# Beta plus x for one group in four: from GpSimd additions to a pair of DMA transfers, with the b2 addition re-divided

## The chip, the core and the metric

The kernel runs on one core of one Trainium2 chip. The metric is the device time of one execution in microseconds (us); lower is better. The engines are TensorE (PE, with its weight loads PEld), VectorE (DVE), ScalarE (ACT), GpSimd (POOL) and SyncE (SP, which here only issues DMAs).

## The reference

`x` has 128 batches of 128 rows by 512 columns, in float32. Each batch `b` has a language id between 0 and 8 (the tables have ten rows), which chooses its weights:

```python
w1 = W1[language_ids]; w2 = W2[language_ids]
h = relu(einsum('bsh,bha->bsa', x, w1) + b1[language_ids][:, None, :])     # 512 -> 128
y = x + einsum('bsa,bah->bsh', h, w2) + b2[language_ids][:, None, :]       # 128 -> 512
mean, var = over the 512 columns of y
normed = (y - mean) * rsqrt(var + 1e-5)
out = x + normed * gamma[language_ids][:, None, :] + beta[language_ids][:, None, :]
```

## The kernel before, in words

All 128 rows of a batch lie on the 128 partitions, so one batch is a 128x512 tile. Input comes in groups of four batches (`G`, one DMA of 1 MB, `load_x`), output goes out in pairs (one DMA of 512 KB, `store`). W1, W2 and the rows of beta, gamma and b2 are held on the chip for all ten languages (`beta_b`, `gamma_b` and `b2_b` have each row copied to every partition), and each engine picks its slice with a register that holds the language id (`lid`).

The work on one batch `b`:

- TensorE transposes x (`transpose_x`, L218), ScalarE copies the transpose out (L222) and copies the batch's W1 to a buffer (`stage_w1`, L209). TensorE multiplies by W1 (`down`, L241), ScalarE adds b1 and applies relu (L249), TensorE multiplies by W2 (`up`, L258).
- The addition of b2 has three ways. For batches that `b2_by_matmul` names, TensorE adds it with one more matmul into the same PSUM tile (L257). For those of `b2_by_vector`, VectorE adds it in PSUM (L271). For all others GpSimd makes `r = x + b2` ahead of time (`add_b2`, L228).
- VectorE adds `r` (or x) to the product in PSUM and sums the row (`residual`, L273). ScalarE makes the sum of squares (L288), VectorE the statistics, then `(y - mean) * gamma` (`scale`, L322), and last `o = y * rstd + o` (`finish`, L331), where `o` already holds `x + beta`.
- That first content of `o`, `x + beta`, is made by GpSimd (`add_beta`, L235) for each batch.

The order on each engine is written out by hand: `keep` (L44) ties each instruction behind the one before it on its engine. Only the stores are issued outside it, so that the builder places them among SP's other DMAs. The main loop (L492) counts `i`, with `b = i - 3`. In the turn of `b`, GpSimd makes `r` of batch b+2 and `o` of batch b, TensorE does `up` of b+1, VectorE does `residual` of b, and `finish` follows three batches behind. For the last five batches (`E` = 123) the order differs: in the turn of 123 GpSimd makes everything that is left of `r` and `o`, and afterwards it takes part in the ends of batches 123, 124 and 125 (`by_pool`, L384 and L386: two multiplications by gamma and three additions, between ScalarE and the stores). The last six stores are of one batch each, and SP issues them in the order of the batches.

The buffers that count here: four `r` tiles (`rp`), so that GpSimd can make the fifth `r` only when VectorE's `residual` has used the first; five `o` tiles of two batches each (`op`), so that the sixth waits for the first one's store to land; five PSUM tiles for the product (`p_y`), so that TensorE's `up` of b+5 waits for `finish` of b; four x tiles of a group each.

Of the kernel before, what the change touches and what calls it, by code (L numbers as in the profile page):

```python
# [8 lines left out]
FP = mybir.dt.float32  # L9
# [3 lines left out]
ALU = mybir.AluOpType  # L13
ET = mybir.EngineType
PSUM = bass.MemoryType.PSUM

P = 128
G = 4
# [6 lines left out]
def cond_resid_kernel(ctx: ExitStack, tc: tile.TileContext, x, itok, W1, b1, W2, b2, gamma, beta, out):  # L25
# [8 lines left out]
    nc = tc.nc  # L34
    B, S, H = x.shape
    L, _, A = W1.shape
    KC = H // P
    NG = B // G
# [5 lines left out]
    def keep(ins):  # L44

        engine = ins.ins.engine
        if engine in last:
            tc.add_manual_dep(ins.ins, last[engine], behind, reason="kept order")
        last[engine] = ins.ins.name
        return ins  # L50
# [1 line left out]
    const = ctx.enter_context(tc.tile_pool(name="const", bufs=1))  # L52
    xp = ctx.enter_context(tc.tile_pool(name="xp", bufs=4))
    rp = ctx.enter_context(tc.tile_pool(name="rp", bufs=4))
    op = ctx.enter_context(tc.tile_pool(name="op", bufs=5))
    tp = ctx.enter_context(tc.tile_pool(name="tp", bufs=2))
    wp = ctx.enter_context(tc.tile_pool(name="wp", bufs=3))
    st = ctx.enter_context(tc.tile_pool(name="st", bufs=6))
# [5 lines left out]
    xs = {}  # L64

    def load_x(g):
        t = xp.tile([P, G, H], FP, tag="x", name=f"x_{g}")
        keep(nc.sync.dma_start(out=t, in_=x[g * G : (g + 1) * G].rearrange("b s h -> s b h")))
        xs[g] = t

    def xb(b):
        return xs[b // G][:, b % G, :]
# [27 lines left out]
    for l in range(0, L, 5):  # L100
        keep(
            nc.sync.dma_start(
                out=w1e[:, l : l + 5].rearrange("p l k a -> p l (k a)"),
                in_=W1[l : l + 5].rearrange("l (p k) a -> p l (k a)", k=KC),
# [4 lines left out]
    def load_w1(k):  # L109
        keep(  # L110
            nc.sync.dma_start(out=w1[:, :, k, :], in_=W1[:, k * P : (k + 1) * P, :].rearrange("l p a -> p l a"))
        )

    for l in range(0, L, 5):
        keep(
            nc.sync.dma_start(
                out=w2[:, l * H : (l + 5) * H].rearrange("p (l h) -> p l h", l=5),
                in_=W2[l : l + 5].rearrange("l a h -> a l h"),
# [48 lines left out]
    beta_b = const.tile([P, L * H], FP, name="beta_b")  # L167
# [14 lines left out]
    lids, xT, w1s, hT, rs, os, ys, ssqs, nmeans, rstds = {}, {}, {}, {}, {}, {}, {}, {}, {}, {}  # L182
    phs, pxs, sums = {}, {}, {}

    def lid(b, engine):
        g = b // G
        if (g, engine) not in lids:
            loads, vals = nc.values_load_multi_w_load_instructions(
                lang[0:1, g * G : (g + 1) * G],
                engines=[engine],  # L190
                min_val=0,
                max_val=L - 1,
                skip_runtime_bounds_check_because="clamped on the chip to 0..L-1 above",
            )
            for ins in loads:
                keep(ins)
            lids[g, engine] = vals
        return lids[g, engine][b % G]

    def b2_by_matmul(b):  # L200
        return b < 4 or (b % 4 == 1 and not b2_by_vector(b))

    def b2_by_vector(b):
        return b % 8 == 5 and 8 <= b < B - 16

    def stage_w1(b):
        w1s[b] = wp.tile([P, KC, A], FP, tag="w1s", name=f"w1s_{b}")
        src = (w1e if b < EARLY else w1).rearrange("p l k a -> p (l k a)")[:, bass.ds(lid(b, ET.Activation) * (KC * A), KC * A)]
        keep(nc.scalar.copy(w1s[b].rearrange("p k a -> p (k a)"), src))  # L209

    def transpose_x(b):
        pxs[b] = p_x.tile([P, KC, P], FP, tag="xT", name=f"pxT_{b}")
        for k in range(KC):
            if b < EARLY:
                cols = xb(b).rearrange("s (p k) -> s k p", k=KC)[:, k, :]
            else:
                cols = xb(b)[:, k * P : (k + 1) * P]
            keep(nc.tensor.transpose(pxs[b][:, k, :], cols, ident))  # L218

    def copy_xT(b):  # L220
        xT[b] = tp.tile([P, KC, P], FP, tag="xT", name=f"xT_{b}")
        keep(nc.scalar.copy(xT[b], pxs.pop(b)))  # L222

    def add_b2(b):
        if not b2_by_matmul(b) and not b2_by_vector(b):
            rs[b] = rp.tile([P, H], FP, tag="r", name=f"r_{b}")
            v = lid(b, ET.Pool)
            keep(nc.gpsimd.tensor_tensor(rs[b], xb(b), b2_b[:, bass.ds(v * H, H)], ALU.add))  # L228

    def add_beta(b):  # L230
        g, j = divmod(b, 2)
        if j == 0:
            os[g] = op.tile([P, 2, H], FP, tag="o", name=f"o_{g}")
        v = lid(b, ET.Pool)
        keep(nc.gpsimd.tensor_tensor(os[g][:, j, :], xb(b), beta_b[:, bass.ds(v * H, H)], ALU.add))  # L235

    def down(b):
        phs[b] = p_h.tile([P, P], FP, tag="h", name=f"ph_{b}")
        for k in range(KC):
            keep(  # L240
                nc.tensor.matmul(  # L241
                    phs[b], lhsT=w1s[b][:, k, :], rhs=xT[b][:, k, :], start=(k == 0), stop=(k == KC - 1)
                )
            )
        del xT[b], w1s[b]

    def relu(b):
        hT[b] = tp.tile([P, P], FP, tag="hT", name=f"hT_{b}", bufs=6)
        keep(nc.scalar.activation(hT[b], phs.pop(b), AF.Relu, bias=b1T[:, bass.ds(lid(b, ET.Activation), 1)]))  # L249

    def up(b):
        v = lid(b, ET.PE)
        ys[b] = p_y.tile([P, H], FP, tag="y", name=f"py_{b}")
        m = b2_by_matmul(b)
        if m:
            pick_b = pick[:, bass.ds(v + 2 * L, 1)].to_broadcast([96, P])
            keep(nc.tensor.matmul(ys[b], lhsT=pick_b, rhs=parts[:96, :], start=True, stop=False))  # L257
        keep(nc.tensor.matmul(ys[b], lhsT=hT[b], rhs=w2[:, bass.ds(v * H, H)], start=not m, stop=True))  # L258
        del hT[b]
# [5 lines left out]
    def residual(b):  # L265
        r = rs.pop(b) if b in rs else xb(b)
        if b % 2 == 0:
            sums[b // 2] = st.tile([P, 2], FP, tag="sum", name=f"sum_{b // 2}")
        if b2_by_vector(b):
            v = lid(b, ET.DVE)  # L270
            keep(nc.vector.tensor_tensor(ys[b], ys[b], b2_b[:, bass.ds(v * H, H)], ALU.add))  # L271
        keep(
            nc.vector.scalar_tensor_tensor(ys[b], ys[b], 1.0, r, ALU.mult, ALU.add, accum_out=col(sums, b))  # L273
        )
# [28 lines left out]
    def rstd_1(g):  # L303
        y0s[g] = p_s.tile([P, 6], FP, tag="s", name=f"stat_{g}")
        keep(nc.vector.reciprocal(y0s[g][:, 0:2], sds[g]))  # L305
# [32 lines left out]
    def on(b):  # L338
        return 0 <= b < B
# [152 lines left out]
    for i in range(3, B + U):  # L492
        b = i - U - 1
        if b > 0 and b % G == 0 and b // G + 3 < NG:
            load_x(b // G + 3)
        if i == 5:
            load_x(3)
        if i in (4, 6, 8, 10):
            load_w1((i - 4) // 2)
        if i == 4:  # L500
            up(2)
        if i == 5:
            up(3)
        if i > 3 and on(i):
            transpose_x(i)
        if b <= E:
            add_b2(b + 2)
            add_beta(b)
        if i > 4 and on(i - 1):
            down(i - 1)  # L510
        if i > 3 and on(i):
            copy_xT(i)
        if i > 4 and on(i + 1):
            stage_w1(i + 1)
        if i > 4 and on(i - 1):
            relu(i - 1)
        if i > 5 and on(i - U):
            up(i - U)


        g, half = divmod(b, 2)
        p = g - 1
        mine, old = 0 <= p < B // 2, 0 <= p - 1 < B // 2
        if b == E:
            add_b2(b + 3)
            add_beta(b + 1)
            add_b2(b + 4)
            for n in range(b + 2, B):
                add_beta(n)
        if b > E:  # L530
            tail(b)
        elif half == 0:
            if on(b):
                residual(b)
            if mine:
                rstd_1(p)
                scale(2 * p)
            if on(b):
                negative_mean(b)
            if mine:  # L540
                rstd_2(p)
            if old:
                finish(2 * p - 1)
                store(p - 1)
            if mine:
                rstd_3(p)
        else:
            if on(b):
                residual(b)
            if mine:  # L550
                rstd_4(p)
                scale(2 * p + 1)
            if on(b):
                negative_mean(b)
            if mine:
                finish(2 * p)
        if 0 <= b <= E:
            square(b)
            if half == 1:
                deviation(g)  # L560

        for n, engine in ((i + 3, ET.Activation), (i - U + 3, ET.PE), (b + 1, ET.DVE), (b + 5, ET.Pool)):
            if on(n):
                lid(n, engine)
# [37 lines left out]
```

## Time and profile before

| | before |
|---|---|
| median of 3 runs | 313.8 us (313.76 to 313.9) |
| the profiled execution: its own time, and its span | 313.83 us, 312.1 us |
| granted TensorE clock | 0.99 |
| PE busy | 300.5 us, 96% |
| DVE busy | 297.3 us, 95% |
| ACT busy | 285.4 us, 91% |
| POOL busy | 280.1 us, 90% |
| GpSimd additions: `r`, `o` | 93 of 1274 ns, 128 of 1274 ns |
| b2 matmuls on TensorE (L257), b2 additions on VectorE (L271) | 22 of 381 ns, 13 of 692 ns |
| DMA, mean | 242 GB/s, 75.49 MB |

The span runs from the first to the last instruction of the profiled execution; the other 1.73 us of its time lie around it. A matmul's duration in the profile reaches over the start of the next one, so that TensorE's pace is read from the distance between starts. The same holds for GpSimd and VectorE, whose instructions overlap a little. Times inside the span are counted from its start.

### The profile page before, as it was taken

Reading aid. Unit: us, or ns where it says so; the run is one execution under the profiler, and the core shown is the slowest. Engines: PE = TensorE matmul, PEld = TensorE weight load, DVE = VectorE, ACT = ScalarE, POOL = GpSimd, SP = SyncE. Lnnn points to the kernel's source line nnn. Section 1 sums busy time; section 2 is a strip of 40 time slices with the busy share of each in tenths; the row PEclk is TensorE's granted clock in tenths of the full one; section 3 lists DMA queues with packets and bytes.
Section 4 is the critical chain, followed back from the end, with each engine's and each line's share of the span. In section 5 each row is a group of like instructions: output and inputs, shape, how many; then the busy total and the mean of one; then the engine's idle time right before and its main releaser. Section 6 shows DMA issues by size and latency. Waiting matters only on the chain.

```text
span 312.1 us, 7096 instructions
## 1 busy us (share of the span) xinstructions
PE 300.5 (96%) x1869; PEld 223.8 (72%) x1869; DVE 297.3 (95%) x945; ACT 285.4 (91%) x724; POOL 280.1 (90%) x234
## 2 busy tenths in 40 slices
PE   8999999999999999999999999999999999999970
PEld 3567787777777767777777777777777777777740
DVE  6677999999999999999999999999999999999995
ACT  3878999999999999999999999999999999999982
POOL 1319978999999999999999999999999999999963
PEclk9999999999999999999999999999999999999995
DMA  6999998767776777667666567576666667633234
GB/s 209 387 387 352 326 339 275 238 229 226 236 250 225 255 265 269 242 231 270 257 227 226 210 238 253 213 272 269 232 232 198 232 247 239 244 134 138 88 149 168
DMA packets 42313, 75.49 MB, mean 242 GB/s; under 512 B 1785, under 2 KB 6916, under 8 KB 42274
## 3 DMA queue, kind: packets, MB, share of 16 engines
q1 hardware_dynamic: 42214, 75.00, 68.6%
q8 instruction: 15, 0.25, 0.3%
q14 instruction: 24, 0.20, 0.2%
q10 hardware_dynamic: 60, 0.05, 0.1%
HBM read 41.49 MB, written 33.55 MB: 240 GB/s over the span
## 4 chain that ended last, share of the span: by engine, by line
PE 91%; DVE 5%; ACT 1%; issue 1%; DVEq 1%; DMA 1%; ACTq 0%
PE ph L241 36%; PE py L258 34%; PE pxT L218 18%; PE py L257 1%; PE row L175 1%; DVE py L273 1%; DVE gamma_b L180 1%; DVE py L322 1%; DVE o L331 1%; DMA rows<-in_L_cond_b_dram 1%; ACT sq L366 0%; DVEq L597 0%; ACT n L382 0%; DVE left L156 0%; DVE left L154 0%
## 5 line engine op out<-in xcount | busy, mean ns | idle before, releaser
L235 POOL TENSOR_TENSOR o<-x,beta_b 128x512 f32<-128x512 f32 x128 | 161.6, 1274 | 12.8 <-ACT beta_b L178 9.2
L241 PE MATMUL ph<-xT,w1s 128*128 128x128 f32 x1024 | 135.6, 275 | 0.5 <-ACT w1s L209 0.5
L258 PE MATMUL py<-w,hT 128*128 x256 | 131.1, 594 | 0.0
L228 POOL TENSOR_TENSOR r<-x,b_b 128x512 f32<-128x512 f32 x93 | 118.5, 1274 | 11.5 <-DMA x<-in_x_dram 9.2
L241 PEld LDWEIGHTS ph<-xT,w1s 128*128 128x128 f32 x1024 | 124.7, 192 | 2.4 <-ACT w1s L209 1.0
L218 PEld LDWEIGHTS pxT<-ident,x 128*128 128x128 f32 x512 | 65.5, 148 | 64.9 <-issue 44.8
L322 DVE SCALAR_TENSOR_TENSOR py<-py,nmean,gamma_b 128x512 f32<-128x512 f32 x126 | 93.8, 745 | 0.2 <-issue 0.2
L331 DVE SCALAR_TENSOR_TENSOR o<-py,rstd,o 128x512 f32<-128x512 f32 x122 | 91.0, 746 | 0.0
L288 ACT ACTIVATE sq<-py,sum 128x512 f32<-128x512 f32 x124 | 85.3, 688 | 1.4 <-DVE py L273 1.3
L222 ACT COPY xT<-pxT 128x512 f32<-128x512 f32 x128 | 73.8, 577 | 9.8 <-PE pxT L218 6.3
L218 PE MATMUL pxT<-ident,x 128*128 128x128 f32 x512 | 77.4, 274 | 0.0
L209 ACT COPY w1s<-w 128x512 f32 x112 | 69.5, 621 | 0.0
L273 DVE SCALAR_TENSOR_TENSOR py<-py,r 128x512 f32<-128x512 f32 x93 | 64.6, 694 | 1.3 <-PE pxT L218 0.6
L249 ACT ACTIVATE hT<-ph,b1T 128x128 f32<-128x128 f32 x128 | 47.4, 370 | 1.0 <-PE ph L241 1.0
L258 PEld LDWEIGHTS py<-w,hT 128*128 128x128 f32 x256 | 40.6, 192 | 2.4 <-ACT hT L249 0.7
L273 DVE SCALAR_TENSOR_TENSOR py<-py,x 128x512 f32<-128x512 f32 x35 | 24.4, 697 | 1.6 <-ACT sq L288 0.6
L288 ACT ACTIVATION_READ_ACCUMULATOR sq<-py,sum 128x1 f32 x124 | 25.7, 208 | 0.0
L299 ACT ACTIVATE sd<-ssq,eps 128x2 f32<-128x2 f32 x62 | 18.3, 296 | 2.1
L279 DVE TENSOR_SCALAR nmean<-sum 128x1 f32<-128x1 f32 x128 | 19.5, 152 | 0.1
L305 DVE RECIPROCAL stat<-sd 128x2 f32<-128x2 f32 x62 | 13.0, 210 | 1.0 <-ACT sd L299 1.0
L273 DVE DVE_READ_ACCUMULATOR py<-py,r 128x1 f32 x93 | 13.4, 144 | 0.0
L317 DVE RECIPROCAL rstd<-stat 128x2 f32<-128x2 f32 x62 | 10.4, 168 | 0.0
(56 smaller groups left out, 120.6 us busy)
## 6 DMA issues: line engine op xcount, KB each, us to landing
out_dram<-o SPq DMA_DIRECT2D x61, 512.0 KB, 3.9
x<-in_x_dram SPq DMA_DIRECT2D x30, 1024.0 KB, 5.8
w1e<-in_L_cond_W_dram SPq DMA_DIRECT2D x2, 1280.0 KB, 8.7
w<-in_L_cond_W_dram SPq DMA_DIRECT2D x2, 1280.0 KB
w<-in_L_cond_W_dram SPq DMA_DIRECT2D x4, 640.0 KB, 15.2
x<-in_x_dram SPq DMA_DIRECT2D x4, 512.0 KB, 8.4
out_dram<-o SPq DMA_DIRECT2D x6, 256.0 KB, 2.0
rows<-in_L_cond_beta_dram ACTq DMA_DIRECT2D x1, 20.0 KB
```

The source lines that it names most:

```text
L209: keep(nc.scalar.copy(w1s[b].rearrange("p k a -> p (k a)"), src))
L218: keep(nc.tensor.transpose(pxs[b][:, k, :], cols, ident))
L222: keep(nc.scalar.copy(xT[b], pxs.pop(b)))
L228: keep(nc.gpsimd.tensor_tensor(rs[b], xb(b), b2_b[:, bass.ds(v * H, H)], ALU.add))
L235: keep(nc.gpsimd.tensor_tensor(os[g][:, j, :], xb(b), beta_b[:, bass.ds(v * H, H)], ALU.add))
L241: nc.tensor.matmul(phs[b], lhsT=w1s[b][:, k, :], rhs=xT[b][:, k, :], start=(k == 0), stop=(k == KC - 1))
L249: keep(nc.scalar.activation(hT[b], phs.pop(b), AF.Relu, bias=b1T[:, bass.ds(lid(b, ET.Activation), 1)]))
L258: keep(nc.tensor.matmul(ys[b], lhsT=hT[b], rhs=w2[:, bass.ds(v * H, H)], start=not m, stop=True))
L273: nc.vector.scalar_tensor_tensor(ys[b], ys[b], 1.0, r, ALU.mult, ALU.add, accum_out=col(sums, b))
L288: nc.scalar.activation(sq, ys[b], AF.Square, bias=col(sums, b), scale=-float(H), accum_out=col(ssqs, b))
L322: nc.vector.scalar_tensor_tensor(ys[b], ys[b], col(nmeans, b), gamma_b[:, bass.ds(v * H, H)], ALU.add, ALU.mult)
L331: nc.vector.scalar_tensor_tensor(o, ys.pop(b), rstds[g][:, j : j + 1], o, ALU.mult, ALU.add)
```

## The change

Every fourth group of batches (q = 3, 7, ... 27, so 7 groups and 28 batches) gets its `x + beta` without GpSimd arithmetic. SP issues four DMAs that copy the rows of beta from `beta_b` to a tile `od` of four batches (`fill_beta`, in the turn five batches ahead of the group), and GpSimd issues one DMA of 1 MB that adds the group's x to that tile as it lands (`add_x`, two batches ahead). The `od` pool has one tile. The pool of `o` tiles goes from five to four.

b2 is re-divided. `b2_by_matmul` keeps batches 0 to 3 alone (22 matmuls become 4). `b2_by_vector` names one batch in 16 in place of one in 8 (21, 37, ... 101: 13 become 6). GpSimd takes the rest (93 become 118). Its `o` additions fall from 128 to 100.

```diff
-    op = ctx.enter_context(tc.tile_pool(name="op", bufs=5))
+    op = ctx.enter_context(tc.tile_pool(name="op", bufs=4))
+    od = ctx.enter_context(tc.tile_pool(name="od", bufs=1))
...
     def b2_by_matmul(b):
-        return b < 4 or (b % 4 == 1 and not b2_by_vector(b))
+        return b < 4

     def b2_by_vector(b):
-        return b % 8 == 5 and 8 <= b < B - 16
+        return b % 16 == 5 and 8 <= b < B - 16
...
+    def beta_by_dma(q):
+
+        return q % 4 == 3 and q < NG - 2
+
+    def fill_beta(q):
+
+        o = od.tile([P, G, H], FP, tag="od", name=f"od_{q}")
+        os[2 * q], os[2 * q + 1] = o[:, 0:2, :], o[:, 2:4, :]
+        for j in range(G):
+            v = lid(q * G + j, ET.SP)
+            keep(nc.sync.dma_start(out=o[:, j, :], in_=beta_b[:, bass.ds(v * H, H)]))
+        return o
+
+    def add_x(q, o):
+        keep(nc.gpsimd.dma_start(out=o, in_=xs[q], accum_op=ALU.add))
+
     def add_beta(b):
         g, j = divmod(b, 2)
+        if beta_by_dma(b // G):
+            return
         if j == 0:
             os[g] = op.tile([P, 2, H], FP, tag="o", name=f"o_{g}")
...
         if i > 3 and on(i):
             transpose_x(i)
+        q, at = divmod(b + 5, G)
+        if at == 0 and beta_by_dma(q):
+            filled = fill_beta(q)
+        q, at = divmod(b + 2, G)
+        if at == 0 and beta_by_dma(q):
+            add_x(q, filled)
         if b <= E:
             add_b2(b + 2)
             add_beta(b)
```

## The prediction

> **What bounds the kernel now.** I read the page's chain first: 91% of it is TensorE. Then TensorE's timeline, where columns are start, duration (us), engine, line, operation, names.
>
> ```profile
> PE 91%; DVE 5%; ACT 1%; issue 1%; DVEq 1%; DMA 1%; ACTq 0%
> ```
> ```profile
> 126.18 1.06 PE L241 MATMUL ph<-xT,w1s 128*128 128x128 f32 x8
> 127.07 1.02 PE L258 MATMUL py<-w,hT 128*128 x2
> 127.93 0.60 PE L218 MATMUL pxT<-ident,x 128*128 128x128 f32 x4
> 128.37 1.06 PE L241 MATMUL ph<-xT,w1s 128*128 128x128 f32 x8
> 129.26 0.38 PE L257 MATMUL py<-parts,pick 96*128 96x512 bf16 x1
> 129.48 1.02 PE L258 MATMUL py<-w,hT 128*128 x2
> 130.34 0.60 PE L218 MATMUL pxT<-ident,x 128*128 128x128 f32 x4
> 130.78 1.06 PE L241 MATMUL ph<-xT,w1s 128*128 128x128 f32 x8
> ```
>
> From L241 to L241 a batch takes 2.19 us; with the b2 matmul 2.41, so that matmul costs 0.22 (its 381 ns overlap the next). TensorE stands back to back. VectorE follows right behind; in its timeline a pair of batches takes 4.24 us (residuals at 126.63, 128.68, 130.86) against TensorE's 4.38, plus 0.72 where it adds b2. ScalarE, 96% busy in the middle, has room too. GpSimd's starts lie 1.234 us apart (32 steps from 95.11 to 134.60): 14 additions in 8 batches are 17.3 us against TensorE's 17.7.
>
> Then the start and the end on GpSimd, where its cover is thin.
>
> ```profile
> 39.60 1.26 POOL L228 TENSOR_TENSOR r<-x,b_b 128x512 f32<-128x512 f32 x1
> 43.12 2.51 POOL L235 TENSOR_TENSOR o<-x,beta_b 128x512 f32<-128x512 f32 x2 [2.25 <-DMA out_dram<-o]
> ...
> 293.72 1.27 POOL L228 TENSOR_TENSOR r<-x,b_b 128x512 f32<-128x512 f32 x1 [0.31 <-DVE stat L305]
> 294.96 3.73 POOL L235 TENSOR_TENSOR o<-x,beta_b 128x512 f32<-128x512 f32 x3
> 300.98 1.27 POOL L384 TENSOR_TENSOR n<-n,gamma_b 128x512 f32<-128x512 f32 x1 [2.28 <-ACT n L382]
> ```
> ```profile
> 34.45 3.90 SPq L335 DMA_DIRECT2D out_dram<-o  x1
> 38.46 0.41 SPq L68 DMA_DIRECT2D x<-in_x_dram  x1
> 38.95 2.82 SPq L335 DMA_DIRECT2D out_dram<-o  x2
> ```
>
> The reader sees that the first store, issued only at 38.35, lands at 43.1 and holds GpSimd; that at the end GpSimd finishes its `o` at 298.7 and idles 2.28 us; and that `r` waits for VectorE, that is, for one of four buffers.
>
> **The Trainium skill.** "DMA: Bandwidth & Descriptors", section "SWDGE vs HWDGE vs iDMA": an accumulating DMA can be issued from GpSimd only, and its cores compute the descriptors in software. The trace of before has no such DMA. Same page, "Specifications": such a DMA's first byte comes after about 1 us, which "Latency and other measured facts" puts down to that work; no run here shows it. Same page, "Anatomy of one DMA — SWDGE (gpsimd) path": 2.0 us plus bytes over 436e3, for 1 MB an estimate of 4.4; the trace's 1 MB loads of x (from SP) take 5.8 (median), and I use that. "SBUF — State Buffer", "Who interferes with whom": VectorE's two-port copies can lock GpSimd out while it writes descriptors; VectorE's wide operations in the loop all read PSUM, so I charge nothing.
>
> **The change, part by part.** T(b) is the start of batch b's residual on VectorE.
>
> *b2 off TensorE.* 18 matmuls go, 17 of them ahead of T(123): 17 x 0.22 = 3.74 us, all on the path. The seven additions that leave VectorE were within its slack: nothing. VectorE now needs 8 x 4.24 + 0.72 = 34.6 us per 16 batches against TensorE's 35.04, so TensorE stays the pace.
>
> *GpSimd, the middle.* Per 16 batches 15 `r` and 12 `o`: 27 x 1.234 = 33.3 us plus X, the issue of the accumulating DMA. X lies between 0.05 (a mere dispatch; it can't gain) and 2 (a core writes read and write descriptors for 128 rows one by one); I take the page's 1.0. 34.3 is under 35.04: GpSimd gains 0.7 per 16 batches until it is at its farthest ahead. Break-even is X = 1.7.
>
> *SP.* Five instructions more per DMA group (a register load and four copies, some 0.4 each by the x row), in all some 2.2 us on a queue that mostly waits; stores behind them have two or more batches of room in the middle. The load of x of group q+4 now waits for the accumulation, and in the built order two stores stand behind it; their `o` buffers are wanted more than 8 batches later. Nothing.
>
> *The start, batches 8 to 13.* Here cover is gone. With 4 `o` tiles it is `o` of batch 8 that waits for the store of 43.1, not batch 10. GpSimd's order from there: o_8 43.1, r_11 44.4, o_9 45.6, free at 46.8. Then comes `add_x` of group 3, in front of r_12. It waits for the four copies, which stand on SP behind the store that is issued until 38.35: issued about 39 to 41.4. They queue behind what SP has in flight: DMA moves about 300 to 350 GB/s then (profile row GB/s), the store lands 43.1, and 0.25 + 0.5 (the next store) + 0.75 MB follow: 1.5 MB at 0.3 MB per us is 5 us. I take 48.1 (46.8 at best, where it waits for nothing; 50.5 with a slower receipt). r_12 then ends at 48.1 + 1.0 + 1.27 = 50.4. T(12) was 48.24, less two b2 matmuls 47.8: VectorE stands 2.6 us. r_13 and r_14 have `o` additions between, and lose 0.3 each. TensorE's `up` needs `finish` of five batches before: `finish` of batch 40 ended at 128.77, `up` of 45 began at 129.26, so 0.5 is cover. TensorE loses 2.6 + 0.6 - 0.5 = 2.7, and never regains it, being the pace.
>
> *The accumulation's transfer* must land before `finish` of batch 12, T(15) + 1.5, some 10 us after the issue. One 1 MB load takes 5.8; a read of both operands bounds it at twice that, 11.6, so 0 to 2 us once. I take 0: each such stand puts GpSimd further ahead next time.
>
> *The end.* From batch 112 on every `r` and `o` is GpSimd's: 2 x 1.234 = 2.47 per batch against 2.19, where before three batches in four had both. At best r_114 starts when a buffer is free: T(110) + 0.83 (before: 293.72 against a residual at 292.89). 30 additions follow: 37.0 us. T(123) is 13 x 2.19 = 28.5 after T(110): GpSimd is free at T(123) + 9.4. Before: T(123) = 295.10, free at 298.7, the first multiplication (L384) at T(123) + 5.9. So the chain of five begins 3.5 later. It took 300.98 to 307.41, 6.43. SP then issues the last three stores in order (3 x 0.37), the last lands 1.7 later and 1.33 more end the span: 4.15. The end is T(123) + 9.4 + 6.43 + 4.15 = 20.0, against 17.0 before: +3.0. The 2.28 us idle was the cover; it is used up.
>
> *Sum*, against the profiled execution's own 313.83 (0.03 over the median): -3.74 + 2.7 + 3.0 = +2.0: **315.8 us**.
>
> **Rivals.**
>
> *A, the start costs little; the time stays about the same.* The copies, from SBUF to SBUF, land by 46.8, and X is small. Then the stand is 48.1 + X - 47.8, less 0.5. With none, 313.83 - 3.74 + 3.0 = 313.1; with X = 1, 313.9. For it: the DMA row falls after 45 us. Against: stores and copies share one queue. It decides from a landing before 47.5: 313.6. This is also the side not slower: the last chain alone then cancels the saving.
>
> *B, GpSimd becomes the bound.* X = 2: 35.3 per 16 batches, more than 35.04. GpSimd never gets ahead (r_114 only 3.8 instead of 6.7 us early, end +2.9), each group stands some 0.3 (1.5 in all), the start costs 1.0 more: 321. X = 1.5 gives 318. A late transfer adds to the same account. It decides from X = 1.25, above which GpSimd isn't at its farthest ahead by batch 114. For it: two operands' descriptors. Against: the page's 1 us.
>
> *C, the end is hidden*, so that the whole saving arrives: 313.83 - 3.74 = about 310. It needs GpSimd more than four `r` ahead, which the buffers exclude.
>
> **How the numbers follow.** Forecast 0.50 (314.5 to 317.5), A 0.27 (313.1 to 314.4), B 0.19 (317.5 to 322), C 0.04. A measurement here tells apart about 0.2%, that is 313.2 and 314.4. Faster: C and 0.06 of A, 0.10. Same: 0.18 of A. Slower: 0.72. Range: from A's lower end, 313.2, to B with X = 2, 321, leaving out C and a little of A and B.
>
> **What would show it.** A wait of `add_x` of group 3 at about 47 to 48, VectorE waiting for GpSimd at batch 12 for 2 to 3 us and nearly nowhere else; the DMA's issue about 1 us; 2.19 per batch between; GpSimd's last chain starting about 9.4 after T(123), with no idle time, and the end of the chain going through L384/L386 and the last stores. It is wrong if GpSimd waits for ScalarE before L384 as before, if the accumulation takes over 10 us to land, or if TensorE's pace is not 2.19.

## The result, and the profile after

The changed kernel takes 342.56 us (median of 4 runs, 341.8 to 344.28) against 313.78 (313.69 to 313.9) on the same chip: 1.0925 times as long, 95% interval 1.0884 to 1.0966. The profiled execution took 342.54 us with a span of 340.8, which is 28.7 more than before. The forecast was 315.8, in a range that ended at 321.

The chain that ended last, on the page of after:

```profile
PE 38%; POOL 22%; issue 12%; DVE 10%; DMA 10%; SPq 3%; POOLq 3%; DVEq 0%
PE py L277 17%; PE ph L260 14%; POOL o L254 10%; POOL r L229 9%; PE pxT L219 7%; DMA od<-beta_b 6%; DMA x<-in_x_dram 4%; DVE py L341 3%; DVE py L292 3%; DVE o L350 3%; POOLq L189 2%; POOL od L245 1%; SPq L117 1%; POOL o L405 1%; POOL n L403 1%
```

TensorE's share fell from 91% to 38%. Not because it became slower: in its timeline of after, a batch still takes 2.19 us from one L260 to the next, and no b2 matmul stands between.

```profile
99.76 1.06 PE L260 MATMUL ph<-xT,w1s 128*128 128x128 f32 x8
100.66 1.02 PE L277 MATMUL py<-w,hT 128*128 x2
101.52 0.60 PE L219 MATMUL pxT<-ident,x 128*128 128x128 f32 x4
101.95 1.06 PE L260 MATMUL ph<-xT,w1s 128*128 128x128 f32 x8
```

It waits instead. From the waits of after (who waited for whom: us in total, times, longest):

```profile
POOL o L254 <- DMA out_dram<-o: 34.0, 12, 4.9
DVE py L292 <- POOL r L229: 26.3, 27, 2.3
PE py L277 <- DVE o L350: 17.1, 16, 1.9
```

Read from the top this is one stall handed on: GpSimd waits until a store has landed so that it may overwrite an `o` tile, VectorE waits for the `r` that GpSimd makes after it, TensorE waits for the PSUM tile that VectorE's `finish` frees. Before, the first line stood at 3.6 us and the second wasn't there. From T(4), the residual of batch 4, on, 16 batches took 37.2, 38.9, 38.3, 39.8, 39.9, 39.1 and 38.4 us, in place of 35.5.

GpSimd's timeline of after, at the start and then in the second DMA group:

```profile
42.92 1.28 POOL L254 TENSOR_TENSOR o<-x,beta_b 128x512 f32<-128x512 f32 x1 [4.53 <-DMA out_dram<-o]
44.16 1.29 POOL L229 TENSOR_TENSOR r<-x,b_b 128x512 f32<-128x512 f32 x1
45.39 1.29 POOL L254 TENSOR_TENSOR o<-x,beta_b 128x512 f32<-128x512 f32 x1
47.72 1.01 POOL L245 DMA_DIRECT2D od<-x  x1 [1.04 <-DMA od<-beta_b]
48.48 1.55 POOL L229 TENSOR_TENSOR r<-x,b_b 128x512 f32<-128x512 f32 x1
...
76.80 1.44 POOL L229 TENSOR_TENSOR r<-x,b_b 128x512 f32<-128x512 f32 x1
83.15 1.28 POOL L254 TENSOR_TENSOR o<-x,beta_b 128x512 f32<-128x512 f32 x1 [4.91 <-DMA out_dram<-o]
...
86.82 0.86 POOL L245 DMA_DIRECT2D od<-x  x1
87.43 1.55 POOL L229 TENSOR_TENSOR r<-x,b_b 128x512 f32<-128x512 f32 x1
```

The first five lines follow the forecast's start: it had 43.1, 44.4, 45.6 and 48.1 for the first four, and 50.4 for the end of `r` of batch 12, which came at 50.03. The line of 83.15 is what it did not have: `o` of batch 24 waits 4.91 us for a store. SP's timeline shows where that store was:

```profile
67.23 0.38 SPq L69 DMA_DIRECT2D x<-in_x_dram  x1
67.71 0.97 SPq L354 DMA_DIRECT2D out_dram<-od  x2
76.31 1.79 SPq L241 DMA_DIRECT2D od<-beta_b  x3
78.19 0.55 SPq L354 DMA_DIRECT2D out_dram<-o  x1
78.88 0.49 SPq L241 DMA_DIRECT2D od<-beta_b  x1
...
106.17 0.38 SPq L69 DMA_DIRECT2D x<-in_x_dram  x1
```

SP issues its DMAs in order, and this is a loop. The load of x at 67.23 waits until GpSimd has read the last of the old x (`o` of batch 19, which ends at 67.2). The two stores of the beta tile stand behind that load, and go at 67.71, though VectorE had finished the first pair at 61.4 (60.68 + 0.74). The copies of beta need the beta tile empty, and wait for those stores to land: 76.31. The store of pair 8 stands behind three of the copies: 78.19, though VectorE had finished it at 69.9. It lands, and at 83.15 GpSimd goes on. From there it works without a pause for 23.0 us, until it has made `o` of batch 35, and then the next load of this kind goes, at 106.17. So once round the loop takes 15.9 us from the load to `o` of batch 24 and 23.0 us of GpSimd's work: 38.9 us for 16 batches, which is the cycle that was measured there, where TensorE needs 35.04. SP's own waits of after name both links:

```profile
SPq L69 <- POOL o L254: 119.4, 13, 11.3
SPq L241 <- DMA out_dram<-od: 40.8, 6, 7.8
```

The last chain of additions on GpSimd began at T(123) + 12.9 (329.85 against 316.95), where 9.4 was forecast, and the span ended 23.8 after T(123), where 20.0 was forecast and it had been 17.0 before. Of the 28.7 us, 21.85 are T(123), which came at 316.95 in place of 295.10, and 6.85 the end.

### The profile page after: what moved, and what is told of

Same layout as the page of the kernel before. It is cut to its first block, busy times and chain, and to the rows that moved or that the text cites. A ratio compares the mean times of both kernels' runs of the same rounds, so it can differ in the third digit from the quotient of the medians.

```text
span 340.8 us, 7091 instructions
## 1 busy us (share of the span) xinstructions
PE 303.9 (89%) x1851; PEld 223.1 (65%) x1851; DVE 293.4 (86%) x938; ACT 288.2 (85%) x724; POOL 282.2 (83%) x238
## 4 chain that ended last, share of the span: by engine, by line
PE 38%; POOL 22%; issue 12%; DVE 10%; DMA 10%; SPq 3%; POOLq 3%; DVEq 0%
PE py L277 17%; PE ph L260 14%; POOL o L254 10%; POOL r L229 9%; PE pxT L219 7%; DMA od<-beta_b 6%; DMA x<-in_x_dram 4%; DVE py L341 3%; DVE py L292 3%; DVE o L350 3%; POOLq L189 2%; POOL od L245 1%; SPq L117 1%; POOL o L405 1%; POOL n L403 1%
## 5 line engine op out<-in xcount | busy, mean ns | idle before, releaser
L254 POOL TENSOR_TENSOR o<-x,beta_b 128x512 f32<-128x512 f32 x100 | 131.5, 1325 | 43.2 <-DMA out_dram<-o 34.0
L229 POOL TENSOR_TENSOR r<-x,b_b 128x512 f32<-128x512 f32 x118 | 155.4, 1345 | 9.1 <-DMA x<-in_x_dram 9.1
L277 PE MATMUL py<-w,hT 128*128 x256 | 134.5, 607 | 17.6 <-DVE o L350 17.1
L260 PE MATMUL ph<-xT,w1s 128*128 128x128 f32 x1024 | 135.6, 275 | 0.5 <-ACT w1s L210 0.5
L260 PEld LDWEIGHTS ph<-xT,w1s 128*128 128x128 f32 x1024 | 124.7, 192 | 2.4 <-ACT hT L268 1.1
L292 DVE SCALAR_TENSOR_TENSOR py<-py,r 128x512 f32<-128x512 f32 x118 | 81.5, 691 | 29.4 <-POOL r L229 26.3
L350 DVE SCALAR_TENSOR_TENSOR o<-py,rstd,o 128x512 f32<-128x512 f32 x94 | 69.7, 742 | 0.0
L277 PEld LDWEIGHTS py<-w,hT 128*128 128x128 f32 x256 | 39.0, 191 | 25.3 <-DVE o L350 23.0
L350 DVE SCALAR_TENSOR_TENSOR od<-py,rstd,od 128x512 f32<-128x512 f32 x28 | 20.8, 743 | 0.0
L292 DVE DVE_READ_ACCUMULATOR py<-py,r 128x1 f32 x118 | 16.5, 140 | 0.0
L336 DVE RECIPROCAL rstd<-stat 128x2 f32<-128x2 f32 x62 | 10.2, 164 | 0.0
```

The costliest lines, as they stand in the source:

```text
L260: nc.tensor.matmul(phs[b], lhsT=w1s[b][:, k, :], rhs=xT[b][:, k, :], start=(k == 0), stop=(k == KC - 1))
L350: nc.vector.scalar_tensor_tensor(o, ys.pop(b), rstds[g][:, j : j + 1], o, ALU.mult, ALU.add)
```

## The experiments

All runs are compared with the kernel before on the same chip (313.74 to 313.81 us). T(123) and the end after it are read from each profile; a "cycle" is 16 batches.

**The order on SP, alone.** Only the stores from pair 4 on are tied into the written order; up to there SP's order is that of the changed kernel.

```diff
-        nc.sync.dma_start(out=out[2 * g : 2 * g + 2].rearrange("b s h -> s b h"), in_=os.pop(g))
+        ins = nc.sync.dma_start(out=out[2 * g : 2 * g + 2].rearrange("b s h -> s b h"), in_=os.pop(g))
+        if g >= 4:
+            keep(ins)
```

> The changed kernel with the stores of the pairs from the fifth on (g >= 4) tied into SP's written order, so that the two stores of pairs 8k and 8k+1 stand ahead of the copies of beta, and the stores of the beta tile ahead of the next load of x; everything else as in the changed kernel. Theory 1 (order on SP: the store whose o buffer GpSimd needs stands behind the copies of beta, and these wait for the beta tile's stores, which stand behind a load of x that waits for GpSimd): a cycle of 16 batches falls from 38.8 us to TensorE's 35.04, the waits of GpSimd for a landed store from 34 us to under 8; T(123) about 293.5, time 314 to 317. Theory 2 (the accumulating DMA itself, its 0.85 us on GpSimd, the slower additions behind it and the fuller DMA engines, whatever the order): the cycle stays above 38 us and the time above 338.

Measured: 318.6 us, 1.0153 times before (1.0133 to 1.0173). Its SP timeline over the same stretch:

```profile
61.93 4.61 SPq L354 DMA_DIRECT2D out_dram<-od  x2
67.33 0.38 SPq L69 DMA_DIRECT2D x<-in_x_dram  x1
70.41 5.34 SPq L354 DMA_DIRECT2D out_dram<-o  x2
76.32 2.45 SPq L241 DMA_DIRECT2D od<-beta_b  x4
```

and two lines of its waits:

```profile
POOL o L254 <- DMA out_dram<-o: 5.4, 2, 4.7
DVE py L292 <- POOL r L229: 2.4, 3, 1.9
```

The copies go at the same moment as in the changed kernel, 76.3, but the stores have gone ahead of them. The cycles after the first fall to 35.2 us on average, T(123) to 294.56, and 24 of the 28.7 us are gone. Theory 1 stands, though its time was 1.6 us too low, and theory 2 falls: the same accumulating DMAs, on DMA engines that move 285 GB/s in place of 265, cost the cycles hardly anything. What is left, 4.5 us of span, is the start and the end.

**Five `o` tiles, with the order left as it was.**

```diff
-    op = ctx.enter_context(tc.tile_pool(name="op", bufs=4))
+    op = ctx.enter_context(tc.tile_pool(name="op", bufs=5))
...
-        hT[b] = tp.tile([P, P], FP, tag="hT", name=f"hT_{b}", bufs=6)
+        hT[b] = tp.tile([P, P], FP, tag="hT", name=f"hT_{b}", bufs=4)
...
-        sq = tp.tile([P, H], FP, tag="sq", name=f"sq_{b}")
+        sq = tp.tile([P, H], FP, tag="sq", name=f"sq_{b}", bufs=1)
```

(the last edit in both places where `sq` is made)

> The changed kernel with five o tiles again in place of four (room made by one tile less for the junk output of the squares and two less for relu's output); the order on SP stays. Theory 1 (a late store hurts only because four tiles make GpSimd wait for the store eight batches back): o of pair 8k+4 then waits for a store long landed, pair 8k+5 for the late one, which has landed just by then: cycle 35.0 to 35.6, time 314 to 318. Theory 2 (the accumulating DMA and the DMA load): cycle above 38 us, time above 338. A third, that one buffer less for the squares costs something: ScalarE's waits grow and the time is over 320.

Measured: 328.57 us, 1.0498 times before (1.0442 to 1.0555). Theories 1 and 2 missed the number on either side. It is over 320, as the third has it, but ScalarE's waits did not grow (10.2 us for VectorE before the squares, 24.8 in the changed kernel). A line of GpSimd's waits and one of VectorE's tell what happened:

```profile
POOL od L245 <- DMA od<-beta_b: 19.8, 6, 5.6
DVE od L350 <- issue: 6.5, 4, 2.0
```

The wait for a store is gone entirely, so the fifth tile does cover it; but the copies are as late as before (SP's wait for the beta tile's stores is 47.7 us in 6), and now GpSimd runs up against them at `add_x`. Theory 1 holds in its cause and missed that the late copies are a second way for the same loop to reach GpSimd. VectorE also stood 6.5 us in four before a `finish` on the beta tile. The waits name no releaser, but each time `add_x` had landed 0.09 us before (at 131.23, 168.06, 206.02 and 243.04), so it is the late `add_x` that lands late. The cycles are 35.6 to 38.0 us from the second on. It is half an answer only, because two other buffers changed as well.

**The DMA part alone**, b2 divided as before:

```diff
     def b2_by_matmul(b):
-        return b < 4
+        return b < 4 or (b % 4 == 1 and not b2_by_vector(b))

     def b2_by_vector(b):
-        return b % 16 == 5 and 8 <= b < B - 16
+        return b % 8 == 5 and 8 <= b < B - 16
```

> The DMA part alone: b2 divided as before (22 matmuls on TensorE, 13 additions on VectorE, 93 on GpSimd), beta by DMA for one group in four, four o tiles. GpSimd then has 24 additions of 1.234 us and one issue per 16 batches, 30.5 us against TensorE's 35.5. Theory 1 (order on SP): the late store still comes by the chain of stores and copies, about 16.5 us after the residual of the fourth batch of the beta tile's successor; GpSimd's room takes up most, but not all of it: 0 to 2 us per cycle, time 315 to 328. Theory 3 (the extra additions of the re-division are the cause, GpSimd being short of time): no stand at all, 313.5 to 315.

Measured: 315.14, 316.56, 322.07 and 324.32 us, so far apart that no ratio is given; all four lie in the range of theory 1. The profiled one is that of 316.56. In it GpSimd waits for stores as long as in the changed kernel:

```profile
POOL o L254 <- DMA out_dram<-o: 32.3, 14, 5.9
DVE py L292 <- POOL r L229: 2.5, 2, 2.0
```

but VectorE hardly waits for GpSimd (2.5 us against 26.3). The late stores are there without the re-division; what hides them is, by all that these lines show, GpSimd's spare time (252.0 us busy in this run, 282.2 in the changed kernel), and the re-division takes that away. Theory 3 is wrong about the waits; that the additions are needed for the loss is right.

**The re-division alone**, with five `o` tiles and no beta by DMA:

```diff
     def beta_by_dma(q):
-
-        return q % 4 == 3 and q < NG - 2
+        return False
```

> The re-division alone: b2 by GpSimd in 15 of 16 batches, all of x + beta on GpSimd too, five o tiles, no beta tile and no DMAs for it. GpSimd has 31 additions per 16 batches, 38.3 us against 35.04, and is the bound from the start: 22.3 + 244 x 1.234 + 3.6 (the store wait at the start) = 327, then the chain of five, 6.4, and the stores, 4.2: span about 337.6, time 339. If it is below 330, additions on GpSimd overlap more than their distance of 1.234 us says.

Measured: 347.04 us, 1.1052 times before (1.1027 to 1.1077). GpSimd is the bound as expected, and most of the 8 us beyond came from waits for stores (10.0 us in 6, of which I had put in 3.6): here, too, loads that wait for GpSimd stand ahead of them (SP's load waited 207.1 us for GpSimd's `o`).

**Four `o` tiles in the kernel before**, alone, and then with the stores from pair 4 on in the written order.

```diff
-    op = ctx.enter_context(tc.tile_pool(name="op", bufs=5))
+    op = ctx.enter_context(tc.tile_pool(name="op", bufs=4))
```

> The kernel before with four o tiles in place of five and nothing else. GpSimd then waits for the store eight batches back in place of ten; in the middle that store has landed about 1 us after the r buffer is free, and GpSimd has the time (17.3 us of additions in 17.7). If the fifth tile matters only beside a late store: 313.7 to 314.6. If four tiles alone hold GpSimd up: over 315.5.

> The kernel before with four o tiles in place of five, as in the run of that alone, and the stores from pair 4 on in SP's written order, so that a load of x, which waits for GpSimd, no longer stands ahead of the store that GpSimd waits for. If the loop GpSimd, load, store, GpSimd is what four tiles cost (355.75 with them alone): the time falls to 313.5 to 316. If four tiles are too few by themselves (a store's 4 us and VectorE's distance): above 330.

Measured: four tiles alone, 355.75 us, 1.1354 times before (1.1293 to 1.1416), worse than the whole change: four tiles alone do hold GpSimd up, far beyond the 315.5 that was named for it. With the order as well, 315.04, 1.0043 (1.0028 to 1.0058). The waits of the first, then its SP timeline:

```profile
POOL o L235 <- DMA out_dram<-o: 49.7, 27, 7.1
```
```profile
70.69 0.38 SPq L68 DMA_DIRECT2D x<-in_x_dram  x1
71.16 0.97 SPq L335 DMA_DIRECT2D out_dram<-o  x2
80.65 0.38 SPq L68 DMA_DIRECT2D x<-in_x_dram  x1
81.12 0.97 SPq L335 DMA_DIRECT2D out_dram<-o  x2
```

The loop is the bare form of the one above: GpSimd's `o`, the load of x that waits for it, the stores behind that load, their landing, GpSimd's next `o`. It takes 10.1 us on average for four batches, which take 8.9 before, and it sets the pace from end to end. So the loop was in the kernel before all along; its fifth tile gave the store two batches more and hid it. The change took that tile away.

**The end.** The order on SP, and b2 of four late batches by matmul again.

```diff
     def b2_by_matmul(b):
-        return b < 4
+        return b < 4 or (b % 4 == 1 and b >= B - 16)
```

> The changed kernel with SP's stores in the written order from pair 4 on, and b2 of batches 113, 117, 121 and 125 again by a matmul. If the last additions on GpSimd set the end (in the run with the stores in order alone the end came 22.0 us after T(123), before the change 17.0): GpSimd is 4 x 1.234 = 4.9 us less behind, three matmuls ahead of T(123) cost 0.66, the end comes about 17 to 18 after T(123) and the time falls from 318.6 to 314 to 315.5. If something else sets it (the last stores, the DMA engines), it stays above 317.5.

Measured: 313.65 us, 0.9996 times before (0.9986 to 1.0007). The end came 16.8 after T(123) (311.4 - 294.60), and T(123) stayed where it was (294.56 without this edit). The end was set by how far GpSimd was behind with its last additions; four fewer remove the delay.

**The start.** The order on SP, no beta by DMA in group 3, five early batches by matmul.

```diff
     def b2_by_matmul(b):
-        return b < 4
+        return b < 4 or (b % 4 == 1 and b < 28 and not b2_by_vector(b))
...
-        return q % 4 == 3 and q < NG - 2
+        return q % 4 == 3 and 3 < q < NG - 2
```

> The changed kernel with SP's stores in the written order from pair 4 on, beta by DMA from group 7 on only (six groups), and b2 of batches 5, 9, 13, 17 and 25 again by a matmul. If the stand at batches 12 to 14 is the fill's wait on a loaded DMA queue plus the store that GpSimd waits for: VectorE's waits there (2.4 us on GpSimd in the run with the stores in order alone) go, five matmuls cost 1.1, the time falls from 318.6 to 316.5 to 317.3. If the start was no cost on the path, it rises by 1.1 to 319.7.

Measured: 318.03 us, 1.014 (1.012 to 1.016), between the two expectations. The stand at batch 12 is gone: T(12) is 48.25 against 50.20. But at T(32) the two stand level, 94.61 and 94.70: the cycle from batch 20 on takes 36.5 us. Without the DMAs of group 3, GpSimd makes nearly every `r` and `o` of the next 16 batches, so that it is short of time there instead; that is argued from its order, as the single waits are small. T(123) is 0.7 us earlier than without this edit, and the intervals of the two times overlap: the stand at the start is gone, but what its going gained in time is not shown.

**All three together**, with all stores in the written order:

```diff
-        nc.sync.dma_start(out=out[2 * g : 2 * g + 2].rearrange("b s h -> s b h"), in_=os.pop(g))
+        keep(nc.sync.dma_start(out=out[2 * g : 2 * g + 2].rearrange("b s h -> s b h"), in_=os.pop(g)))
...
-        return b < 4
+        return b < 4 or (b % 4 == 1 and (b < 28 or b >= B - 16) and not b2_by_vector(b))
...
-        return q % 4 == 3 and q < NG - 2
+        return q % 4 == 3 and 3 < q < NG - 2
```

> All stores in SP's written order, beta by DMA for six groups from group 7 on, and b2 by matmul for one batch in four (less those of VectorE) below 28 and from 112 on. If order, start and end are separate terms: 318.6 less 4.3 (end) less 1.6 (start) = 312.7, so 312 to 313.3, 0.2% to 0.6% faster than before the change. If one is not what I take it for, above 313.8.

> The kernel before with all stores in SP's written order and nothing else: a control for the run that was faster than before. Where five tiles cover the store's delay the order costs and gains nothing: 313.5 to 314.1, so that what that run gained comes from the matmuls taken off TensorE. If the order alone brings the gain: 311.5 to 312.5.

Measured: 311.85 us, 0.9941 times before (0.9927 to 0.9954), faster than both kernels and just under the expected 312 to 313.3. GpSimd again idles before its last chain, as it did before the change:

```profile
298.66 1.27 POOL L403 TENSOR_TENSOR n<-n,gamma_b 128x512 f32<-128x512 f32 x1 [0.38 <-ACT n L401]
```

The control, the kernel before with the same order of stores, is 314.49, 1.0021 (1.0014 to 1.0028), a little above what was expected. So the gain is not the order's; it goes with the nine matmuls fewer on TensorE (13 in place of 22), whose cycles are 35.05 to 35.27 us from the third on, where they were 35.4 to 35.7 before.

That start, end and order are separate terms, as the expectation had it, is not shown. This kernel has one thing more than the runs of its parts: the stores of pairs 0 to 3 are in order too. At the start GpSimd waits 2.7 us for the first store that it needs, where it waited 7.3 in the run of the start alone, and T(36) comes at 101.51 in place of 103.09. The early order is therefore a likely part of the gain, and no run has it alone in the changed kernel.

## Why the prediction was wrong, step by step

- *b2 off TensorE, -3.74.* Not separable in the changed kernel, where TensorE waits; with the order repaired the cycle is 35.2 us on average, where 35.04 was forecast, and T(123) 294.56, where -3.74 + 2.7 from 295.10 gives 294.1. Right.
- *GpSimd, the middle: additions 1.234 apart, the issue 1.0.* Right: the distance stayed 1.23, the issue took 0.85 (median of 7). The 1 us of the Trainium skill ("DMA: Bandwidth & Descriptors", "Specifications") is said of the first byte and not of GpSimd's own time, but it was a fair stand-in. That GpSimd would gain 0.7 per cycle was not so even in the repaired order: it waited 5.9 us at `add_x` in the seven groups, more than the 4.9 of that gain, though the profile names the copies as releaser for 0.8 of them alone.
- *SP: "Five instructions more per DMA group ... Nothing."* **This is the step that failed.** The forecast had seen that stores stand behind the load that waits for the accumulation, and compared them with the batch that next wants their tile. It left out that the beta tile's stores stand behind another load, which waits for GpSimd; that the copies wait for those stores; and that a store of an ordinary pair stands behind the copies. And it granted four tiles two or more batches of room in the middle, where four tiles alone cost the kernel before 42 us. The sign that it named, VectorE waiting for GpSimd at batch 12 and nearly nowhere else, did not come: VectorE waited 27 times, 26.3 us in all. The orders with and without this link differ by 22.4 us at T(123) (316.95 and 294.56) and 1.8 at the end (23.8 and 22.0): 24 of the 27 us between forecast and result.
- *The start, +2.7.* `add_x` was forecast to go at 48.1 and went at 47.72; VectorE's stand at batch 12 was 2.6 and is 2.29. Right. (Where the forecast reads TensorE's cover, it names batches 40 and 45; in the trace they are 44 and 49, and the 0.5 is as read.)

```profile
50.06 0.70 DVE L292 SCALAR_TENSOR_TENSOR py<-py,r 128x512 f32<-128x512 f32 x1 [2.29 <-POOL r L229]
```

- *The accumulation's transfer, 0 to 2 us once.* It landed in 9.4 us (median; the slowest of seven 10.75, which was 0.09 us before `finish` of batch 12 began), so there was no stand in the changed kernel. But the room was thin: with the order repaired it took 10.1 to 12.3, over the 10 us that the forecast had named as a sign against it, and VectorE stood 0.9 us once; with five tiles it stood the 6.5 us above.
- *The end, +3.0.* The mechanism was right, the term too small: 5.0 with the order repaired (22.0 after T(123), against 17.0). The last chain on GpSimd began 11.1 after T(123) in place of 9.4. The forecast put GpSimd farthest ahead at batch 114, r_114 at T(110) + 0.83; it began at 268.75 (the fifth of a row from 263.82), T(110) + 2.45, GpSimd having gained nothing in the cycles. The sum was also half a microsecond short in itself: from the chain's start it reckons 6.43 + 4.15 = 10.6 to the end, and the trace of before has 11.1 there (312.1 - 300.98).
- *The rivals.* None had the loop. B asked whether GpSimd becomes the bound through its own work; it became part of a bound through what it waits for.

Left open: why the runs of the DMA part alone scatter, which one profile doesn't tell, what five tiles with the order repaired would bring, which was not tried, and how the last 2 us of the repaired kernel divide between the start, the end and the first four stores.

## What to carry to other kernels

A queue that issues its DMAs in order, as SP does in the timelines above, makes each of its waits everybody's wait. Before counting a buffer's slack in batches, write down for the queue, in its built order, what each DMA waits for and who waits for its landing, and look for a closed loop; its length in microseconds against the batches that it spans is a bound of its own, which no engine's busy share shows. A buffer that seems spare may be what keeps such a loop off the path: taking it away alone, as an experiment, is cheap and tells.

## What the runs showed of the hardware

- After an accumulating DMA that GpSimd issues, its additions last 1.55 us in the profile in place of 1.28 (48.48 and 87.43). They shrink slowly (1.44 at the 24th, at 76.80) and are 1.28 at once after GpSimd has waited (83.15), while their starts stay about 1.23 apart throughout (48.48, 49.72, 50.94, 52.17). Duration and pace part company here: what GpSimd gets done is read from the distance. Who waits for one addition waits for its end, though: `r` of batch 12 ended at 48.48 + 1.55, and the `residual` followed at 50.06.
- A DMA that adds 1 MB of x onto 1 MB in SBUF lands in 9.4 us (10.6 with the order repaired), a load of 1 MB beside it in 6.6, a copy of 256 KB within SBUF in 2.4. The fit of the Trainium skill ("DMA: Bandwidth & Descriptors", "Anatomy of one DMA — SWDGE (gpsimd) path") gives an estimate of 4.4 for 1 MB; it doesn't speak of accumulation, and the measurement decides.
